# Reordering a software-pipelined attention slot: transposes first, values and division ahead of the last products, norms ahead of the scores

## The chip, the core and the metric

The kernel runs on one core of a Trainium2 chip. The metric is device time in microseconds (us) of one execution, from the launch to the end, as the median of several runs. A profile of one execution goes with it: its span runs from the first to the last instruction.

Five engines work side by side, each through its own instructions in the order in which the kernel wrote them: TensorE (PE; its weight loads, PEld, overlap its matmuls), VectorE (DVE), ScalarE (ACT), GpSimd (POOL) and SyncE (SP), which here issues nearly all DMAs. An instruction that waits holds everything behind it on its engine.

## What is computed

The reference takes x of shape (8, 512, 128) in fp32 and has two parts.

1. A recurrence over the 512 positions, `h = tanh(h A' + x_t B')`, `y = h C'`, whose output is normalised and added to x.
2. Six layers, each an attention and a feed-forward part, each with a residual. The attention has 16 heads of width 64. Queries and keys are scaled to length one, multiplied with learned scales and rotated (rotary embedding with a scale). Every window of 32 queries looks at its own 32 keys and the 32 before them:

```
sim  = einsum('bhwie,bhwje->bhwij', bq, bk2) * 8.0      # 32 x 64 per window, masked
attn = softmax(sim, -1)
out  = einsum('bhwij,bhwje->bhwie', attn, bv2)          # then @ Wo
```

The feed-forward part centres and normalises x, forms `hg = xn @ W1 + b1` with 2 x 341 columns, and adds `(a * gelu(gate)) @ W2 + b2`.

## The kernel before

**Groups.** A group is 8 heads of one batch row (two groups per row, 16 per layer, 96 in all); in layer 0 it is 8 heads of one chunk of 128 positions of four batch rows. `GP = 4` pairs of heads make a group's 128x512 tiles.

**Slots.** The main loop (L1073 to L1097) walks over groups n and, within a group, over four slots t = 0 to 3, one for each 128 query positions. `slot(n, t, feed)` (L952) writes out by hand what every engine does, for several groups at once. `cur` is group n, `one` is n+1, `two` is n+2, `old` is n-1. `last` is the quarter before (t-1 of `cur`, or quarter 3 of `old`), and `back` is the quarter two before.

A quarter of `cur` goes through these steps:

- `mask` (L613): ACT copies the mask into the two PSUM banks `sc`, one quarter ahead.
- `scores` (L623): 64 small PE matmuls add the products of queries and keys to it.
- `less_max` (L636, L639): DVE takes the row maximum and subtracts it into `e` (one buffer).
- `exps` (L646): ACT, in place in `e`.
- One slot later, `turn` (L652, L657): PE transposes `e` into `tp`, ACT copies it to `eT` (one buffer).
- `average` (L670): 64 PE matmuls of `eT` with the values (with a column of ones) into two banks `av`.
- `divide` (L687, L688): DVE takes the reciprocal of the row sum and multiplies, into `ao` (one buffer).
- Another slot later, `turn_back` (L699, L703): PE transposes `ao` into `at`, ACT copies it to `aoT`.
- At t = 1 of the next group, `project` (L708) multiplies all of `aoT` with Wo into `yo`, and `add` (L719) adds it to x.

**Pieces of the groups to come** fill the gaps between these steps. They stand in five lists `fill[0]` to `fill[4]`, which `run(0)` to `run(4)` call:

- t = 0: `one.sums` (L426, `nsq`: sums of squares, then the DVE step x at L441) in `run(0)`; `one.values(0)` and the ten-step reciprocal root `one.inv.solve()` (L446 to L452, DVE) in `run(1)`; `values(1)` in `run(2)`; `values(2)` in `run(3)`. `values` is PE L583 and the ACT copy L592 into `vbuf`.
- t = 1: `one.spread` (L461, `bc`: the reciprocal roots spread over the partitions, four banks) and `one.finish(0)` (DVE L561, then four DMAs on SP) in `run(1)`; `finish(1)` to `finish(3)` later; `old.project` in `run(3)`.
- t = 2 and t = 3: two units of `two`, each `unit_a` (PE L522 `rawa`, ACT L526, DVE L512) and `unit_b` (PE L534 `rawb`, ACT L538 and L540, then POOL L544 and L545); at t = 3 also `one.values(3)` in `run(4)`.

**PSUM.** The pool `mm` has four banks (three during the recurrence); `nsq`, `bc`, `yo`, `rawa`, `rawb`, `vps` and the feed-forward tiles take them in turn. `tp`, `at` and the two `av` take turns in two banks of the pool `acc` (L168). So `tp` waits until `divide` has read the first `av` of the slot before, `at` until it has read the second, and `av` in turn until ACT has copied `tp` and `at`.

**Feed-forward.** Eleven of the groups carry a `Feed` over four batch rows in their slots: `centre` (L828) at t = 0, `sums` and `inv.solve` at t = 1, `apply` (L856) at t = 2. `apply` spreads the roots (`bc_f`), scales four tiles (L859) and then runs the matmuls `fa`, `fg` (L879, L883), the Gelu (ACT L891), the product (DVE L897) and `yf` (L905). A last Feed stands behind the groups.

**Recurrence.** Until group `NREC = 9` the 512 steps of the recurrence run beside the groups: every helper ends in `rec.tick(us)`, which puts one step (a PE matmul L291, an ACT tanh L299) into both queues when enough work has passed. `rec.need` runs the remaining steps of a chunk alone where a group needs its result. There `exps` stands behind `run(2)`, and the fourth `bc` is made after the first three, for want of a bank.

Of the kernel before, what the change touches and what calls it, by code (L numbers as in the profile page):

```python
# [48 lines left out]
def mk_seq_preln_kernel(  # L49
# [112 lines left out]
    with tc.tile_pool(name="qk", bufs=2) as qkp, tc.tile_pool(  # L162
# [634 lines left out]
        class Feed:  # L797
# [55 lines left out]
                        c = slice(3 * h + k, 3 * h + k + 1)  # L853
                        nc.vector.tensor_add(self.b1[:kn, c], bp[:kn, c], self.b1[:kn, c])

            def apply(self):  # L856
                bcs = self.inv.spread(range(GP), f"f{self.nm}")
                for j in range(GP):
                    nc.vector.scalar_tensor_tensor(  # L859
                        self.ctr[j],  # L860
                        bcs[j],
                        par_sb[:, self.l, 4:5],
                        self.ctr[j],
                        ALU.mult,
                        ALU.mult,
                    )
                prs = {}
                for j in range(GP):
                    for k in range(len(KC)):
                        self.hidden(j, k, prs)  # L870
                        if k == 0 and j > 0:
                            self.output(j - 1, prs)
                self.output(GP - 1, prs)
# [53 lines left out]
        NREC = 9  # L927
# [3 lines left out]
        def begin(n):  # L931
            nonlocal xs
            l, b, g = todo[n]
            buf = (n // 2) % 2
            if l == 0:
                c, h = b
                if g == 0:
                    rec.need(c)
                    xs = shifted_chunk(c, h, buf)
                groups[n] = ChunkGroup(n, c, h, g, xs)  # L940
                return
            if n < GL + 4 and g == 0:
                nc.vector.memset(xbufs[buf][D // 2 :, WINDOW : WINDOW + 1], 0.0)
            if g == 0:
                xs = shifted(b, buf)
            groups[n] = Group(n, l, b, g, xs)
# [5 lines left out]
        def slot(n, t, feed=None):  # L952

            cur, one, two = groups.get(n), groups.get(n + 1), None
            old = groups.get(n - 1)
            if n + 2 < len(todo):
                if t == 1 or n + 2 not in groups:
                    begin(n + 2)  # L960
                two = groups.get(n + 2)
            last, lt = (cur, t - 1) if t > 0 else (old, NT - 1)
            back, bt = (cur, t - 2) if t > 1 else (old, NT - 2 + t)
            fill = [[] for _ in range(5)]
            if one and t == 0:
                fill[0] = [one.sums]
                fill[1] = [lambda: one.values(0), lambda: one.inv.solve()]
                fill[2] = [lambda: one.values(1), lambda: one.between(0)]
                fill[3] = [lambda: one.values(2)]
            if feed and t == 0:  # L970
                fill[4] = fill[2] + fill[3]
                fill[2] = [lambda: feed.centre((0, 1))]
                fill[3] = [lambda: feed.centre((2, 3))]
            if one and t == 1:
                fill[1] = [lambda: one.spread(range(4)), lambda: one.finish(0)]
                if n < NREC:

                    fill[1] = [lambda: one.spread((0, 1, 2)), lambda: one.finish(0)]
                    fill[2] = [lambda: one.spread((3,))]
            if feed and t == 1:  # L980
                fill[0] += [feed.sums]
            if old and t == 1:
                fill[3] = [lambda: old.project(wo)]
            if two and t >= 2:
                u = 2 * t - 4
                fill[0] = [lambda: two.unit_a(u)]
                fill[1] = [lambda: two.unit_b(u)]
                fill[2] = [lambda: two.unit_a(u + 1)]
                fill[3] = [lambda: two.unit_b(u + 1)]
            if one and t == 3:  # L990
                fill[4] = [lambda: one.values(3), lambda: one.between(1)]
            if feed and t == 2:
                fill[4] = fill[2] + fill[3]
                fill[3] = fill[1]
                fill[2] = fill[0]
                fill[0], fill[1] = [], [lambda: one.values(3), lambda: one.between(1)]
            if feed and t == 3:
                fill[4] = []

            def run(k):  # L1000
                for f in fill[k]:
                    f()
                if t != 1 or k == 0:
                    rec.piece()
                elif k < 4:
                    rec.piece(False)

            run(0)
            if cur:
                cur.scores(t)  # L1010
            if last:
                last.turn(lt)
            if back:
                back.turn_back(bt)
            run(1)
            if feed and t == 2:
                feed.apply()
            if cur:
                cur.less_max(t)
            if feed and t == 1:  # L1020
                feed.inv.solve()
            if cur and n >= NREC:
                cur.exps()
            run(2)
            if cur and n < NREC:
                cur.exps()
            if cur and t + 1 < NT:
                cur.mask(t + 1)
            elif one and t == NT - 1:
                one.mask(0)  # L1030
            if one and t == 1:
                one.finish(1)
            if last:
                last.average(lt)
            if one and t == 1 and not feed:
                one.finish(2)
                one.finish(3)
            run(3)
            if last:
                last.divide(lt)  # L1040
            if feed and t == 1:
                one.finish(2)
                one.finish(3)
            run(4)
            if old and t == 1:
                old.add()
            if one and t == 3 and renew(n + 1):
                l, _, g = todo[n + 1]
                wv[g] = load_v(l + 1, g)
            if two and t == 3 and renew(n + 2):  # L1050
                l, _, g = todo[n + 2]
                wqk[g] = load_qk(l + 1, g)
            if one and t == 3 and one.l == 0:
                one.keep()

        with tc.manual_schedule():
            ahead = rec.first(0)
            for f in ahead:
                f()
            ahead = [f for c in range(1, NT) for f in rec.first(c)]  # L1060
            while rec.t < P:
                if rec.t % 8 == 7 and ahead:
                    ahead.pop(0)()
                rec.step()
            for _ in range(2):
                rec.piece()
            while rec.posted == 0:
                rec.piece()
                rec.step()
            for t in (2, 3):  # L1070
                slot(-2, t)
            feed = soon = None
            for n in range(-1, len(todo) + 1):  # L1073
                m, l = n % GL, n // GL
                if n == NREC:
                    rec.need(NT - 1)
                    recs.close()
                    mmp = mms.enter_context(tc.tile_pool(name="mm", bufs=4, space=PSUM))
                    ffn_w = load_ffn_weights(0)
                for t in range(NT):  # L1080
                    if t == 3 and n < len(todo) - 1:
                        if n == 12 or (m == 8 and l > 0):
                            soon = Feed(l, 0, ffn_w)
                            soon.biases()
                            biases = soon.b1
                            soon.shift()
                        if m == 0 and l > 0:
                            soon = Feed(l - 1, GP, ffn_w)
                            soon.b1 = biases
                            soon.shift()  # L1090
                    slot(n, t, feed)
                    if feed and t == 2 and feed.b0 == GP:
                        ffn_w = load_ffn_weights(feed.l + 1)
                feed, soon = soon, None
                old = groups.pop(n - 1, None)
                if old and old.n % GL == GL - 1 and old.n + 1 < len(todo):
                    wo = load_wo(old.l + 1)  # L1097
            feed = Feed(DEPTH - 1, GP, ffn_w)
            feed.b1 = biases
            feed.shift()  # L1100
            feed.centre(range(GP))
            feed.sums()
            feed.inv.solve()
            feed.apply()

        for b in range(B):
# [114 lines left out]
```

## Time and profile before

| what | value |
|---|---|
| median of three runs | 3921.19 us (3915.84 to 3924.16) |
| the profiled execution's own time | 3917.3 us |
| its span | 3915.5 us, 158605 instructions |
| mean granted TensorE clock | 0.970 |
| DVE busy | 2543.4 us (65%), 5208 instructions |
| ACT busy | 1933.8 us (49%), 3864 instructions |
| POOL busy | 1825.3 us (47%), 780 instructions |
| HBM read and written | 34.56 MB and 14.20 MB |

How to read the profile lines: in a timeline, a line has the start (us from the span's start), the time, the engine, the source line, the operation, output and input by the program's names with the buffer numbers left out, and how many instructions are merged. In brackets stands the idle time of the engine ahead of the line and what ended it. Names with c0h to c3h belong to layer 0. A PE line's time includes the drain of its last matmul, so that the step from one line's start to the next line's start is what a group of matmuls takes.

### The profile page before, as it was taken

What the parts mean: (1) busy time and instruction counts of PE and PEld (TensorE: products, weight loads), DVE (VectorE), ACT (ScalarE), POOL (GpSimd) and SP (SyncE); (2) the same over time, 40 slices, a digit from 0 to 9 for tenths busy, and PEclk for the clock granted to TensorE, in tenths of its full rate; (3) what the DMA queues carried; (4) which work ended last, traced back from release to release, by engine and by line L of the source; (5) the groups of instructions that cost most, each with busy time, mean ns of one, the idle gap of its engine ahead of it and who ended that gap; (6) DMA issues with size and microseconds to landing.
All of it is one profiled execution on the core that took longest, in us unless ns stands there. A gap on an engine that the chain in (4) does not pass through costs nothing.

```text
span 3915.5 us, 158605 instructions
## 1 busy us (share of the span) xinstructions
PE 3536.6 (90%) x69816; PEld 2164.5 (55%) x69816; DVE 2543.4 (65%) x5208; ACT 1933.8 (49%) x3864; POOL 1825.3 (47%) x780
## 2 busy tenths in 40 slices
PE   5797987999999999999999999999999999999997
PEld 4565655555555555555555455555555555555553
DVE  3355565766677677677677677577677677677673
ACT  1253443545455455455455455455455455455452
POOL 0152341535365356366366366366365355355350
PEclk9897987999999999999999999999999999999998
DMA  3152433554345355355345345255345355354342
GB/s 108 28 116 64 110 79 78 123 128 92 86 113 118 72 117 129 85 113 120 68 112 134 78 109 119 66 117 132 76 111 117 69 128 123 77 118 111 74 110 60
DMA packets 366076, 390.50 MB, mean 100 GB/s; under 512 B 96846, under 2 KB 262220, under 8 KB 365260
## 3 DMA queue, kind: packets, MB, share of 16 engines
q1 hardware_dynamic: 364380, 378.09, 42.2%
q8 instruction: 551, 9.03, 1.0%
q10 hardware_dynamic: 1008, 2.27, 0.2%
q14 instruction: 137, 1.12, 0.1%
HBM read 34.56 MB, written 14.20 MB: 12 GB/s over the span
## 4 chain that ended last, share of the span: by engine, by line
PE 69%; DVE 17%; ACT 8%; issue 4%; DMA 2%; SPq 1%; ACTq 0%; DVEq 0%; POOL 0%
PE sc L623 6%; PE yo L708 6%; PE rawb L534 5%; PE vps L583 5%; PE tp L652 5%; PE rawa L522 5%; PE xb L291 4%; PE nsq L426 4%; PE at L699 4%; PE fa L879 3%; PE yf L905 3%; DVE t L561 3%; PE fg L883 3%; DVE t L512 3%; PE av L670 2%
## 5 line engine op out<-in xcount | busy, mean ns | idle before, releaser
L544 POOL TENSOR_TENSOR u<-rope_sb,bs 128x1024 f32<-128x1024 f32 x320 | 765.9, 2394 | 1347.2 <-ACT bs L540 1168.7
L545 POOL TENSOR_TENSOR t<-t,u 128x1024 f32<-128x1024 f32 x320 | 756.9, 2365 | 25.1
L561 DVE TENSOR_TENSOR t<-t,bc 128x1024 f32<-128x1024 f32 x320 | 376.4, 1215 | 286.8 <-PE bc L461 286.7
L512 DVE SCALAR_TENSOR_TENSOR t<-rawa,par_sb,rope_sb 128x1024 f32<-128x1024 f32 x320 | 409.6, 1280 | 203.3 <-ACT sq L526 196.6
L646 ACT ACTIVATE e<-e 128x512 f32<-128x512 f32 x320 | 201.7, 630 | 432.7 <-DVE e L639 318.2
L657 ACT COPY eT<-tp 128x512 f32<-128x512 f32 x320 | 187.6, 586 | 454.2 <-PE tp L652 454.2
L623 PEld LDWEIGHTS sc<-kbuf,qT 64*32 64x32 f32 x20480 | 226.4, 105 | 257.5 <-ACT sc L613 161.8
L623 PE MATMUL sc<-kbuf,qT 64*32 64x64 f32 x20480 | 280.4, 224 | 85.5 <-ACT sc L613 83.4
L534 PE MATMUL rawb<-xbuf,wqk 128*128 128x512 f32 x640 | 343.9, 619 | 0.0
L708 PE MATMUL yo<-aoT,wo 128*128 128x512 f32 x640 | 298.4, 609 | 35.4 <-DVE t L561 34.3
L522 PE MATMUL rawa<-xbuf,wqk 128*128 128x512 f32 x640 | 328.3, 594 | 1.7 <-DVE t L512 1.7
L583 PE MATMUL vps<-wv,xbuf 128*64 128x256 f32 x2560 | 329.7, 389 | 0.0
L670 PEld LDWEIGHTS av<-vbuf,eT 64*32 64x32 f32 x20480 | 226.9, 105 | 180.5 <-ACT sq L538 110.7
L291 PEld LDWEIGHTS xb<-hT,s1w 128*128 128x128 f32 x1022 | 202.8, 237 | 186.6 <-ACT hT L299 128.6
L670 PE MATMUL av<-vbuf,eT 64*32 64x65 f32 x20480 | 283.4, 225 | 13.0 <-issue 9.8
L688 DVE TENSOR_TENSOR ao<-av,rc 128x256 f32<-128x256 f32 x640 | 271.8, 425 | 22.0
L291 PE MATMUL xb<-hT,s1w 128*128 128x8 f32 x1022 | 223.3, 291 | 57.1 <-ACT hT L299 57.1
L526 ACT ACTIVATE sq<-rawa 128x512 f32<-128x512 f32 x320 | 190.4, 595 | 152.9 <-PE rawa L522 152.9
L299 ACT ACTIVATE hT<-xb 128x8 f32<-128x8 f32 x512 | 91.9, 179 | 329.2 <-PE xb L291 313.7
L652 PE MATMUL tp<-ident,e 128*128 128x128 f32 x1280 | 206.1, 284 | 44.1 <-DVE rc L687 43.2
L583 PEld LDWEIGHTS vps<-wv,xbuf 128*64 128x64 f32 x2560 | 162.4, 136 | 139.5 <-issue 64.4
L639 DVE TENSOR_TENSOR e<-sc,mx 128x512 f32<-128x512 f32 x320 | 221.4, 692 | 27.6 <-PE rawa L522 0.5
(280 smaller groups left out, 6176.4 us busy)
## 6 DMA issues: line engine op xcount, KB each, us to landing
qT<-t SPq DMA_DIRECT2D x640, 128.0 KB
kbuf<-t SPq DMA_DIRECT2D x640, 128.0 KB
vbuf<-vbuf SPq DMA_DIRECT2D x544, 130.0 KB
vbuf<-vbuf SPq DMA_DIRECT2D x160, 97.5 KB
xbuf<-xT SPq DMA_DIRECT2D x95, 128.0 KB
xbuf<-xT SPq DMA_DIRECT2D x80, 127.8 KB
wqk<-in_w_qkv SPq DMA_DIRECT2D x12, 512.0 KB
xf<-xT SPq DMA_DIRECT2D x24, 256.0 KB
```

Of the source, the lines that this page charges most:

```text
L291: nc.tensor.matmul(self.xb[:, k, :], abc[:, 0, :], self.hT[:, (t - 1) % P, :], start=False, stop=True, skip_group_check=True,)
L512: nc.vector.scalar_tensor_tensor(t, self.twice(raw), scale, self.rope(isk, 1), ALU.mult, ALU.mult)
L522: nc.tensor.matmul(raw, self.wqk[:, c, 0], self.xs[:, WINDOW:], start=True, stop=True)
L534: nc.tensor.matmul(raw, self.wqk[:, c, 1], self.xs[:, WINDOW:], start=True, stop=True)
L544: nc.gpsimd.tensor_mul(self.wide(u), self.rope(isk, 0), self.twice(bs))
L545: nc.gpsimd.tensor_add(self.ts[c], self.ts[c], u)
L561: nc.vector.tensor_mul(t, t, self.bcs[c].unsqueeze(1).to_broadcast([P, 2, S]))
L583: nc.tensor.matmul(ps[par * KB : (par + 1) * KB, j], self.xs[:, k0 : k0 + KB], self.wv[:, par * GP * DH : (par + 1) * GP * DH], start=True ...
L623: nc.tensor.matmul(self.sc[blk * QB : (blk + 1) * QB, par, i, :], self.qT[rows, i, q0 : q0 + QB], kT[rows, i, :], start=False, stop=True, ...
L652: nc.tensor.transpose(tp[:, i, :], self.e[:, i].rearrange("p a k -> p (a k)"), ident)
L670: nc.tensor.matmul(av[blk * QB : (blk + 1) * QB, i, :VW], self.eT[rows, i, blk * QB : (blk + 1) * QB], self.v[rows, BT * t + blk, i, :], s ...
L708: nc.tensor.matmul(self.yp, wo[:, self.g * GP + c, :], self.aoT[:, c, :], start=(c == 0), stop=(c == GP - 1),)
```

## The change

The steps of a slot are put into another order, and the Feed's `apply` is cut into `scale` (spread and scaling) and `apply` (the matmuls).

- `turn` and `turn_back` come first, ahead of `run(0)` and `scores`.
- `average`, `less_max`, `exps` and `divide` follow `run(1)`; before, `average` stood behind `run(2)` and `divide` behind `run(3)`.
- At t = 1, `spread` and `finish(0)` move from `run(1)` to `run(0)`, ahead of the scores; `finish(1)` comes behind `divide`.
- In a group with a Feed, `feed.sums` moves from `run(0)` to `run(2)` at t = 1, with `inv.solve` behind it; at t = 2 `feed.scale` is `run(0)` and `feed.apply` is `run(3)`, behind `less_max`, `exps`, `average` and `divide` of that slot, which before stood behind it or around it.

```diff
-            def apply(self):
+            def scale(self):
                 bcs = self.inv.spread(range(GP), f"f{self.nm}")
                 for j in range(GP):
                     nc.vector.scalar_tensor_tensor(
...
+
+            def apply(self):
                 prs = {}
...
             if one and t == 1:
-                fill[1] = [lambda: one.spread(range(4)), lambda: one.finish(0)]
-                if n < NREC:
-
-                    fill[1] = [lambda: one.spread((0, 1, 2)), lambda: one.finish(0)]
+                cs = (0, 1, 2) if tight else range(4)
+                fill[0] = [lambda: one.spread(cs), lambda: one.finish(0)]
+                if tight:
                     fill[2] = [lambda: one.spread((3,))]
             if feed and t == 1:
-                fill[0] += [feed.sums]
+                fill[2] += [feed.sums]
...
             if feed and t == 2:
-                fill[4] = fill[2] + fill[3]
-                fill[3] = fill[1]
-                fill[2] = fill[0]
-                fill[0], fill[1] = [], [lambda: one.values(3), lambda: one.between(1)]
+                fill[4] = fill[0] + fill[1] + fill[2] + fill[3]
+                fill[0], fill[1] = [feed.scale], []
+                fill[2] = [lambda: one.values(3), lambda: one.between(1)]
+                fill[3] = [feed.apply]
...
-            run(0)
-            if cur:
-                cur.scores(t)
             if last:
                 last.turn(lt)
             if back:
                 back.turn_back(bt)
+            run(0)
+            if cur:
+                cur.scores(t)
             run(1)
-            if feed and t == 2:
-                feed.apply()
+            if last:
+                last.average(lt)
             if cur:
                 cur.less_max(t)
-            if feed and t == 1:
-                feed.inv.solve()
-            if cur and n >= NREC:
-                cur.exps()
+                if not tight:
+                    cur.exps()
+            if last:
+                last.divide(lt)
+            if one and t == 1:
+                one.finish(1)
             run(2)
-            if cur and n < NREC:
+            if cur and tight:
                 cur.exps()
             if cur and t + 1 < NT:
                 cur.mask(t + 1)
             elif one and t == NT - 1:
                 one.mask(0)
+            if feed and t == 1:
+                feed.inv.solve()
             if one and t == 1:
-                one.finish(1)
-            if last:
-                last.average(lt)
-            if one and t == 1 and not feed:
                 one.finish(2)
                 one.finish(3)
             run(3)
-            if last:
-                last.divide(lt)
-            if feed and t == 1:
-                one.finish(2)
-                one.finish(3)
             run(4)
```

Here `tight` stands for `n < NREC`. Behind the last group, `feed.scale()` is called ahead of `feed.apply()`.

## The prediction

> **What bounds the kernel now.** I read the page's shares of busy time first, then the chain that ended last, then the timeline of one ordinary group, engine by engine.
>
> ```profile
> PE 3536.6 (90%) x69816; PEld 2164.5 (55%) x69816; DVE 2543.4 (65%) x5208; ACT 1933.8 (49%) x3864; POOL 1825.3 (47%) x780
> PE 69%; DVE 17%; ACT 8%; issue 4%; DMA 2%; SPq 1%; ACTq 0%; DVEq 0%; POOL 0%
> ```
>
> TensorE is the bound, with waits on DVE and ACT strung into its chain. An order can only win those waits. Where they lie shows the PE timeline of one ordinary group (the projection's start recurs every 30.90 us, 1203.98 to 1234.88):
>
> ```profile
> 1199.63 0.86 PE L623 MATMUL sc<-kbuf,qT 64*32 64x64 f32 x64 [1.12 <-ACT sc L613]
> 1201.44 1.17 PE L461 MATMUL bc<-k,selt_sb 32*128 32x128 f32 x32
> 1203.98 3.70 PE L708 MATMUL yo<-aoT,wo 128*128 128x512 f32 x8 [0.57 <-DVE t L561]
> 1207.52 1.02 PE L522 MATMUL rawa<-xbuf,wqk 128*128 128x512 f32 x2
> 1213.92 1.02 PE L522 MATMUL rawa<-xbuf,wqk 128*128 128x512 f32 x2
> 1216.14 0.63 PE L652 MATMUL tp<-ident,e 128*128 128x128 f32 x4 [0.42 <-DVE rc L687]
> 1221.83 1.95 PE L426 MATMUL nsq<-sq,sel_sb 128*32 128x128 f32 x64
> ```
>
> Slots begin at 1199.63 (t=1), 1207.52 (t=2), 1213.92 (t=3), 1221.83 (t=0). They last 7.89, 6.40, 7.91 and, until the next t=1 at 1230.53, 8.70. Three waits, 1.12 + 0.57 + 0.42 = 2.11 us, leave 28.8 of pure TensorE work. The longest comes from a chain over DVE and ACT in t=0:
>
> ```profile
> 1223.86 0.29 DVE L441 TENSOR_SCALAR x<-nsq 128x128 f32<-128x128 f32 x1 [1.04 <-PE nsq L426]
> 1227.31 0.68 DVE L636 TENSOR_REDUCE mx<-sc 128x8 f32<-128x512 f32 x1
> 1228.10 0.69 DVE L639 TENSOR_TENSOR e<-sc,mx 128x512 f32<-128x512 f32 x1
> ```
> ```profile
> 1228.88 0.63 ACT L646 ACTIVATE e<-e 128x512 f32<-128x512 f32 x1 [1.62 <-DVE rc L687]
> 1229.42 0.57 ACT L592 COPY vbuf<-vps 128x512 f32<-128x512 f32 x1
> 1229.88 0.59 ACT L613 CAST sc<-mask_sb 128x512 f32<-128x512 bf16 x1
> ```
>
> The sums of squares start at 1221.83. x follows 2.03 later, ten steps of the root, the maximum, the subtraction, and the exponential 7.05 after the sums' start. A copy and the mask stand behind it, and only then may the next scores start.
>
> **The ordinary group, slot by slot.** No instruction is added or removed; only waits and orders change. Steps below are differences of starts in these timelines.
>
> *t=0.* The two transposes (0.55 + 0.50) now stand ahead of the sums, so the whole chain is 1.05 later: exponential at 8.10, end 8.73. The next slot starts with `tp`, which needs the exponential, not the mask: it starts at about 8.80 instead of 8.70. TensorE's own work in the slot is 7.45, so a wait of 1.35 takes the place of the mask's 1.12: **+0.10**.
>
> *t=1.* Transposes 1.03, `bc` 1.11, scores 0.80, `av` 0.80, projection 3.50. `bc`'s fourth bank holds the values copied last: ACT's queue (exponential, copy 0.54 later, mask 0.47, copy 0.52, 0.59 long) frees it 1.4 after the slot's start, where `bc` wants it at 1.24, so 0.2 is lost. `finish(0)` starts 1.26 after `bc` and ends at 3.7; the projection wants its bank at 3.94, so the 0.57 is gone. Sum 7.45 against 7.89: **-0.44**. What is late next is DVE: `finish(0)`, maximum, subtraction, division, three more `finish` of 1.13 and the addition end at 10.05, which is 2.6 into t=2.
>
> *t=2.* TensorE's work is 6.38 (`tp` 0.55, `at` 0.46, units 0.95 + 0.95 + 0.86 + 0.95, scores 0.85, `av` 0.80). `rawa` starts at 1.02; its square on ACT 1.05 later, DVE's product 0.63 after that, at 2.70 (DVE is free at 2.6). The maximum follows 1.20 later, the subtraction 0.78, the exponential 0.79, ending at 6.10. The next `tp` comes at 6.38, 0.28 later. No wait, **-0.02**, but this margin is the plan's thinnest place.
>
> *t=3.* ACT now carries two squares, a scaling, a mask behind each exponential and is free 1.7 into t=3, so `eT` and the square of `rawa` come 0.7 later than in t=2 and the exponential ends at 6.8. The values' product of 1.0 makes this slot 7.48 long, which covers it. The wait of `tp` for the division (0.42) is gone, since the division now ends in its own slot: **-0.43** against 7.91.
>
> Sum 30.11 against 30.90, -0.79 a group. Groups 9 to 93 without a Feed are 74: **-58 us**. SP gets its DMAs in the same order, `finish(0)`'s earlier in the slot; POOL's four units (4.75 each) stay within 24 us of the 30, so neither queue ends a wait.
>
> **The groups with a Feed** (eleven). Before, from sums to sums, 71.26 (1284.31 to 1355.57):
>
> ```profile
> 1301.30 3.70 PE L708 MATMUL yo<-aoT,wo 128*128 128x512 f32 x8 [0.57 <-DVE t L561]
> 1307.47 0.63 PE L652 MATMUL tp<-ident,e 128*128 128x128 f32 x4 [1.68 <-DVE rc L687]
> 1312.58 1.12 PE L879 MATMUL fa<-xf,w 128*128 128x512 f32 x2 [0.64 <-DVE xf L859]
> 1316.68 1.09 PE L879 MATMUL fa<-xf,w 128*85 128x512 f32 x2 [0.40 <-ACT gl L891]
> ```
>
> Now four things stand in each other's way. Counting from the slot's `tp`:
> 1. The exponential at 8.10 has nine copies of ACT behind it (before: at 7.05). The last values' copy ends at 14.1, and `bc`, moved ahead, waits for that bank: it ends at 15.0.
> 2. `finish(1)` stands behind the division and starts at 18.7, so the projection, which takes its bank, starts at 20.0 instead of 17.0: **+3.0**, a wait of 2.0 for the 0.57 shown.
> 3. `feed.scale` takes the bank of the projection, so it waits for `finish(2)`, `finish(3)` and the addition, until 26.2; from there scaling, scores, `av`, values, and `fa` at 30.2. From the projection's end to `fa` it is 6.7 against 7.65 (1304.93 to 1312.58): **-1.0**.
> 4. The exponential, a copy and the mask now stand on ACT ahead of the Gelu's table and first two Gelus; the fifth matmul pair waits for them 1.65 instead of 0.40: **+1.2**. Behind the Feed a slot without scores and `av` is 0.8 shorter: **-0.8**.
>
> Sum +2.4, times 11: **+26 us**.
>
> **The recurrence** (about nine groups). Before, TensorE runs gapless but for one place:
>
> ```profile
> 344.35 1.15 PE L461 MATMUL bc_c0h<-k_c0h,selt_sb 32*128 32x128 f32 x8 [1.05 <-DVE t_c0h L561]
> 346.87 2.05 PE L708 MATMUL yo_c0h<-aoT_c0h,wo 128*128 128x512 f32 x2
> ```
>
> That 1.05 goes (scores and `av` stand between), but the projection now waits for `finish(1)` behind the division, some 2 us: together nothing. In t=2 and t=3 the exponential stands behind the second square, and the next slot's `tp` needs it 8.2 after the slot's start, where TensorE is there at 7.96. The tanh of the steps queue behind that backlog: 0.24 + 0.57 + 0.4, about 1.2 a group: **+11 us**.
>
> Total -58 + 26 + 11 = -21: 3917.3 becomes 3896.3. The median of the runs lies 3.9 above the profiled execution, so **3900 us**.
>
> **Unknown costs.** A `tp` that waits directly for an exponential is in no row; from below it costs nothing (margin 0.28 holds), from above what `tp` waits elsewhere, 1.68, per slot. I take nothing, as ACT and DVE rows give the ends to 0.1. For the Feed I bound from -0.6 (the 0.57 goes as in ordinary groups) to +4.5 (waits 2 and 4 with no credit for 3); I take the sum. For the recurrence 0 to 2.2 (a wait as long as the projection's in each group).
>
> **A rule that speaks against it.** The granted clock was 1.00 from 1307 to 1313 us, behind the wait of 1.68 and eight transposes, and 0.50 in the empty stretch 304 to 327. The Trainium skill, page "TensorE: Matmul & The Clock Gate", sections "What's actually happening" and "Part 4: PE-mode transpose", says that the clock halves after an idle window of about 3.4 us and that transposes don't count as work. The new order puts waits right against transposes: 1.35 + 1.05 in each group stays under the window, the Feed's `tp`, `at` and wait for banks come near it. By the rule a lost window would cost up to 1.7 us, an estimate from that page, eleven times 19. The row shows none, and my sum has none.
>
> **Rivals.**
> - *B, the Feed loses little* (1 instead of 2.4) and the recurrence nothing: -58 + 11 = -47, 3874. For it: the waits in the Feed overlap, and PE has 1.68 to give. Against: the bank order is fixed.
> - *C, all is given back*: the Feed costs 4, the recurrence 2.2 a group: -58 + 44 + 20 = +6, 3927. This is also the case in which the change does not do what it says: the wait on the mask comes back under the name of the exponential.
> - *D, slower*: ACT's queue in t=2 and t=3 is the new bound. ACT carries ten operations, about 5.3 us, in a slot of 6.4, in order, between a DVE chain of 5.3. Every delay beyond 0.28 in t=2 makes `tp` wait, which delays `eT`, the next square, the next maximum. At 0.6 beyond it, 74 groups lose 44: +23, 3944. It decides from 0.3 beyond, where the total crosses zero. For it: ACT's rows show waits for DVE of 318 us at the exponential. Against: every step above was taken from a row.
>
> **Chances.** Forecast 0.45 (3885 to 3913), B 0.20 (3860 to 3885), C 0.15 (3913 to 3929), D 0.20 (above). A measurement tells 0.2%, 7.8 us. Faster is the forecast with B, 0.65; same is C, 0.15; slower is D, 0.20. The range for 8 in 10 reaches from B's 3868 to D's 3938.
>
> **What would show it.** Right: `sc` has no wait on L613 at t=1; `tp` there waits about 1.3 for the exponential (L646); `yo` and the `tp` of t=3 have no wait in ordinary groups; the projections lie 30.1 apart; in Feed groups `yo` waits about 2 for L561 and group time is near 73.7. Wrong: `tp` waits at the start of t=3 (then D), or a granted clock under 1.00 in the Feed groups, or a period of 30.5 and more.

## The result and the profile after

The changed kernel takes 3943.77 us (median, 3938.76 to 3947.89) where the kernel before took 3918.52 in the same series (3912.38 to 3924.16). The ratio is 1.0064, 95% interval 1.0043 to 1.0085: **slower by 0.6%**, where 3900 and faster was forecast, and 6 us beyond the top of the range. The profiled execution took 3945.58, span 3943.8, mean clock 0.972 (before 0.970).

The page of the changed kernel, its shares of busy time and its chain:

```profile
PE 3555.5 (90%) x69816; PEld 2196.7 (56%) x69816; DVE 2565.5 (65%) x5208; ACT 1902.9 (48%) x3864; POOL 1825.3 (46%) x780
PE 71%; DVE 15%; ACT 6%; issue 6%; DMA 1%; SPq 1%; POOL 0%; DVEq 0%; ACTq 0%
```

DVE and ACT have given up 4 points of the chain, as the change wants it. But "issue", time in which TensorE waits for nothing that the profile shows, went from 4 to 6%. Which instructions it falls on stands in the page's groups: the V products, first in the kernel before, then after (the last columns are the idle time ahead of the group and what ended most of it).

```profile
L670 PE MATMUL av<-vbuf,eT 64*32 64x65 f32 x20480 | 283.4, 225 | 13.0 <-issue 9.8
```
```profile
L670 PE MATMUL av<-vbuf,eT 64*32 64x65 f32 x20480 | 302.1, 225 | 56.7 <-issue 55.9
```

Between 1000 and 3880 us TensorE idles for 197 us before and 185 after (the same stretch of time, not of work: the changed kernel is up to 30 us behind in it). Gone are the mask (82 to nothing), the division (43 to 1), most of `finish` (34 to 13). In their place stand the exponential (76.5) and issue (11 to 76).

An ordinary group of the changed kernel in which nothing is missing, TensorE's timeline (start, time, ...; the order of the last `sc` and the first `av` is blurred because modelled ends overlap):

```profile
1237.54 1.95 PE L426 MATMUL nsq<-sq,sel_sb 128*32 128x128 f32 x64
...
1245.20 0.66 PE L652 MATMUL tp<-ident,e 128*128 128x128 f32 x4 [1.15 <-ACT e L646]
1245.69 0.60 PE L699 MATMUL at<-ident,ao 128*128 128x128 f32 x4
1246.22 1.61 PE L461 MATMUL bc<-k,selt_sb 32*128 32x128 f32 x32
1247.76 0.80 PE L623 MATMUL sc<-kbuf,qT 64*32 64x64 f32 x60
...
1248.42 0.91 PE L670 MATMUL av<-vbuf,eT 64*32 64x65 f32 x62
1249.26 3.70 PE L708 MATMUL yo<-aoT,wo 128*128 128x512 f32 x8
```

This is what the prediction drew: no wait of `sc` for the mask, 1.15 of `tp` for the exponential, none of `yo`. From its sums to the next it is 29.96 (30.11 was forecast, 30.89 is the median before; the shortest is 29.93). The group ahead of it, in the same stretch:

```profile
1215.30 1.61 PE L461 MATMUL bc<-k,selt_sb 32*128 32x128 f32 x32
...
1217.50 0.43 PE L670 MATMUL av<-vbuf,eT 64*32 64x65 f32 x21
1218.71 0.67 PE L670 MATMUL av<-vbuf,eT 64*32 64x65 f32 x41 [0.78 <-issue]
1219.31 1.13 PE L708 MATMUL yo<-aoT,wo 128*128 128x512 f32 x2
```

From `bc` to `yo` 4.01 instead of 3.04, for the same instructions. Of 69 ordinary groups behind 930 us 42 are of this kind ("stalled" below; the others "clean"); the stretch takes 3.00 to 3.07 in the clean ones and 3.46 to 5.07 in the stalled ones, 47.5 us over 3.03 in all.

| from the sums of one group to those of the next, summed | before | after | difference | forecast |
|---|---|---|---|---|
| sums behind the recurrence start at | 665.1 | 676.5 | +11.4 | +11 |
| 11 groups with a Feed | 793.1 | 806.5 | +13.4 | +26 |
| 75 ordinary groups | 2331.7 | 2337.3 | +5.6 | -58 |
| the end, behind the last sums | 125.5 | 123.4 | -2.1 | 0 |

The error is in the third row: it is 64 us off, of which the Feed groups give 13 back. Had all 75 been as long as the shortest, it would be -72 (75 x (29.93 - 30.89)).

**What "issue" is.** The table of DMA queues has one for TensorE's instructions (packets, MB, share of 16 engines):

```profile
q8 instruction: 551, 9.03, 1.0%
```

9.03 MB in 551 packets are 16 KB each. The trace has 141025 records of TensorE (matmuls, weight loads, semaphore waits); over 551 that is 256 a packet. So the instructions come in blocks of 256, that is 128 matmuls with their weight loads. Two facts of the trace tie the waits to these packets. Of the 64 issue waits over 0.5 us between 1000 and 3880 us, 61 end 1.1 to 1.8 us after the end of such a packet (median 1.39), and all 11 in the kernel before do. And no two packets of the queue start less than 3.28 us apart in any of the 14 traces, though the 128 matmuls of `sc` and `av` back to back, with their weight loads as many instructions as a packet holds, take 1.6.

The Trainium skill has the frame: page "Runtime: NRT & Kernel Launch", section "Instruction fetch mechanics", says that the instructions are refilled in blocks of 16 KB, 256 instructions, by a DMA queue that the engine's sequencer drives while it executes the block before, and that this is mostly hidden. Blocks, their size and the queue agree with the trace; that it is hidden does not hold here.

In the kernel before, the transposes stood between the scores and the V products:

```profile
1200.42 0.66 PE L652 MATMUL tp<-ident,e 128*128 128x128 f32 x4
1200.91 0.60 PE L699 MATMUL at<-ident,ao 128*128 128x128 f32 x4
1201.44 1.17 PE L461 MATMUL bc<-k,selt_sb 32*128 32x128 f32 x32
1202.55 0.86 PE L670 MATMUL av<-vbuf,eT 64*32 64x65 f32 x64
```

**Theory T1**: from `bc` to the last `av`, 320 instructions now stand back to back and take 2.7 us. That is faster than instructions arrive, so if a block ends in an unlucky place, TensorE runs dry. **T2**: the fetch is slow because of the DMAs that `finish(0)` now starts at this moment. **T3**: rival D of the prediction, ACT's queue is the bound and issue is a side effect.

### The profile page after: what moved, and what is told of

The parts are those of the page before. It is cut to its first block, busy times and chain, and to the rows that moved or that the text cites. A ratio compares the mean times of both kernels' runs of the same rounds, so it can differ in the third digit from the quotient of the medians.

```text
span 3943.8 us, 158206 instructions
## 1 busy us (share of the span) xinstructions
PE 3555.5 (90%) x69816; PEld 2196.7 (56%) x69816; DVE 2565.5 (65%) x5208; ACT 1902.9 (48%) x3864; POOL 1825.3 (46%) x780
## 3 DMA queue, kind: packets, MB, share of 16 engines
q8 instruction: 551, 9.03, 1.0%
## 4 chain that ended last, share of the span: by engine, by line
PE 71%; DVE 15%; ACT 6%; issue 6%; DMA 1%; SPq 1%; POOL 0%; DVEq 0%; ACTq 0%
PE rawa L522 7%; PE rawb L534 7%; PE yo L708 6%; PE sc L623 5%; PE av L670 4%; PE tp L652 4%; PE xb L291 4%; PE nsq L426 4%; PE at L699 3%; PE bc L461 3%; PE yf L907 3%; PE vps L583 3%; PE fa L881 3%; PE fg L885 3%; DVE e L639 2%
## 5 line engine op out<-in xcount | busy, mean ns | idle before, releaser
L670 PEld LDWEIGHTS av<-vbuf,eT 64*32 64x32 f32 x20480 | 239.5, 105 | 205.8 <-issue 155.1
L670 PE MATMUL av<-vbuf,eT 64*32 64x65 f32 x20480 | 302.1, 225 | 56.7 <-issue 55.9
L522 PE MATMUL rawa<-xbuf,wqk 128*128 128x512 f32 x640 | 342.8, 617 | 0.0
L708 PE MATMUL yo<-aoT,wo 128*128 128x512 f32 x640 | 306.7, 623 | 18.6 <-issue 8.9
L652 PEld LDWEIGHTS tp<-ident,e 128*128 128x128 f32 x1280 | 145.5, 141 | 233.1 <-ACT e L646 144.5
L592 ACT COPY vbuf<-vps 128x512 f32<-128x512 f32 x320 | 186.4, 588 | 176.1 <-PE vps L583 176.1
L538 ACT ACTIVATE sq<-rawb 128x512 f32<-128x512 f32 x320 | 190.7, 596 | 142.8 <-PE rawb L534 142.2
```

What stands on the lines that cost most here:

```text
L522: nc.tensor.matmul(raw, self.wqk[:, c, 0], self.xs[:, WINDOW:], start=True, stop=True)
L652: nc.tensor.transpose(tp[:, i, :], self.e[:, i].rearrange("p a k -> p (a k)"), ident)
L670: nc.tensor.matmul(av[blk * QB : (blk + 1) * QB, i, :VW], self.eT[rows, i, blk * QB : (blk + 1) * QB], self.v[rows, BT * t + blk, i, :], s ...
L708: nc.tensor.matmul(self.yp, wo[:, self.g * GP + c, :], self.aoT[:, c, :], start=(c == 0), stop=(c == GP - 1),)
```

## The experiments

Medians of 4 to 6 runs, ratio to the kernel before of the same series with its 95% interval. "Ordinary" is the mean of 69 groups (sums to sums), "best" the shortest of them, "issue" TensorE's issue waits between 1000 and 3880 us. The diffs of the experiments are shortened; conditions such as "only from group 9 on" or "not in groups with a Feed" stand in the expectations.

| kernel | us | ratio to before | ordinary (best) | issue |
|---|---|---|---|---|
| before | 3918.52 | 1 | 30.96 (30.89) | 11 |
| changed | 3943.77 | 1.0064 (1.0043 to 1.0085) | 30.96 (29.93) | 76 |
| e1_split_project | 3964.32 | 1.0117 (1.0097 to 1.0137) | 31.28 (31.01) | 34 |
| e2_close_t0 | 3962.06 | 1.0109 (1.0088 to 1.0130) | 31.14 (29.95) | 75 |
| e3_old_rec | 3944.03 | 1.0062 (1.0044 to 1.0080) | 31.08 (29.94) | 75 |
| e4_old_feed | 3966.61 | 1.0124 (1.0103 to 1.0144) | 30.94 (29.72) | 64 |
| e5_spread_early | 3853.91 | 0.9826 (0.9810 to 0.9842) | 29.75 (29.09) | 42 |
| e6_early_split | 3854.81 | 0.9830 (0.9814 to 0.9845) | 29.78 (29.30) | 35 |
| e7_shift | 3952.45 | 1.0078 (1.0061 to 1.0095) | 31.02 (29.92) | 76 |
| e8_early_split_old_rec | 3847.52 | 0.9809 (0.9791 to 0.9826) | 29.76 (29.30) | 31 |
| e9_values_between | 3836.55 | 0.9776 (0.9760 to 0.9793) | 29.60 (29.30) | 24 |
| e10_spread_behind_scores | 3956.45 | 1.0083 (1.0068 to 1.0098) | 31.13 (30.24) | 79 |
| e11_feed_finish | 3846.79 | 0.9806 (0.9792 to 0.9820) | 29.76 (29.31) | 27 |
| e12_at_between | 4036.73 | 1.0292 (1.0275 to 1.0310) | 32.31 (31.34) | 14 |

**e1, the run cut in two.**

```diff
-    fill[0] = [one.spread(range(4)), one.finish(0)]
-    fill[3] = [old.project(wo)]
+    fill[0] = [one.spread((0, 1, 2)), one.finish(0)]
+    fill[1] = [old.project(wo, (0, 1))]        # ahead of average
+    fill[2] = [old.project(wo, (2, 3)), one.spread((3,))]
```

> The changed kernel, but in ordinary groups (n >= 9, no Feed) half of the projection (yo) stands at t=1 between the scores and the V products, the other half behind these; three of the four bc are spread ahead of the scores and the fourth behind the projection, so that yo finds a free bank. Theory T1 (PE's instructions run out where bc, sc and av stand back to back: 320 records of matmuls and weight loads in 2.7 us): the issue waits between 1000 and 3880 us fall from 76 to below 35, ordinary groups last 30.0 to 30.5 instead of 31.1, the whole 3885 to 3912. T2 (the instruction fetch is slowed by the DMAs that finish(0) starts at that moment, not by the density): issue waits stay above 60 and the time at 3936 to 3952. T3 (ACT's queue in t=2 and t=3 is the bound, as in rival D of the prediction): tp waits at the start of t=3 and t=0 stay, the time at 3936 to 3952 or longer.

The waits went as T1 says: 76 to 34, and of 36 waits of `av` right behind `sc` three are left. The time went the other way, and the timeline shows why:

```profile
1216.47 1.17 PE L461 MATMUL bc<-k,selt_sb 32*128 32x128 f32 x24
1217.57 0.86 PE L623 MATMUL sc<-kbuf,qT 64*32 64x64 f32 x64
1218.36 1.99 PE L709 MATMUL yo<-aoT,wo 128*128 128x512 f32 x4
1220.27 0.86 PE L670 MATMUL av<-vbuf,eT 64*32 64x65 f32 x64
1221.06 1.98 PE L709 MATMUL yo<-aoT,wo 128*128 128x512 f32 x4
1222.98 1.15 PE L461 MATMUL bc<-k,selt_sb 32*128 32x128 f32 x8
```

The 24 `bc` take 1.10 to the next start, as long as all 32 did, and the 8 set apart take 1.08 once more. The four row groups of `bc` run beside each other, so that one alone costs as much as four. That is the experiment's own price: 29.93 + 1.08 = 31.01, its best group. So e1 speaks for T1 by its waits, and its time tells nothing against it.

**e2, another run made dense.** At t=0 the first `vps` goes ahead of the scores, which puts `sc` and `av` together.

```diff
-    fill[0] = [one.sums]
-    fill[1] = [one.values(0), one.inv.solve()]
+    fill[0] = [one.sums, one.values(0)]
+    fill[1] = [one.inv.solve()]
```

> The changed kernel, but at t=0 the first values product (vps) stands ahead of the scores, so that sums (64 matmuls), then 8, then scores and V products (128) stand back to back; nothing is added. T1: at t=0 the issue waits rise from some 13 of 1.0 us to 35 or more, and the whole to 3958 to 3990. T2 (DMAs): t=0 starts no finish; issue waits and time stay, 3936 to 3952. T3: the same, no change.

The time came out as T1 had it, but not for its reason: the issue waits did not rise, 75 against 76. A run of 256 instructions between slower ones, 1.6 us long, made t=0 stall in 15 of 70 groups, no more than the 16 of the changed kernel, while the run of 320 at t=1 stalls in 42. Of the 18 us more, 8 lie ahead of 930 us and 12 in the ordinary groups; what they are is not shown.

**e3 and e4, the old order in the recurrence, and in the Feed groups.** The old `slot` is called where `n < NREC`, or where the group has a Feed.

> The order of before in all groups n < 9 (the recurrence), the changed order behind them. The step of the prediction (+11 for the recurrence): the first sums of 64 matmuls after the recurrence start at 665 instead of 676.5, the whole 3944 - 11 = 3933 (3926 to 3939). Rival: the recurrence is paced by its own chain and regains the loss, 3944.

> The order of before in all four slots of the eleven groups with a Feed, the changed order elsewhere. If the Feed groups lose 13.4 as the two traces say: 3944 - 13 = 3931 (3924 to 3936), each Feed group near 72. If the clean +2.4 of the prediction is the price: 3944 - 26 = 3918. Rival: the issue waits only move into these groups, 3944.

In e3 the first sums behind the recurrence come 9.5 earlier (667.1 against 676.5 in the changed kernel) and those of the first ordinary group behind 930 us 12.0 (938.5 against 950.5): the step is right. But the whole did not move: 8 of it went in the ordinary groups. Their instruction supply is not the reason, since the issue waits are the same, 75 against 76; the waits of `tp` for the exponential rose from 76.5 to 82.7, and the cause of the loss stays open. e4 missed by its seams. Its Feed groups last 74.7, longer than in either kernel, for the old order divides at the end of a slot and the new one begins the next with `tp`, which needs that division. The waits of TensorE in e4 (us in total, times, longest):

```profile
PE tp L652 <- DVE rc L687: 33.1, 20, 1.7
```

So parts of the change that look separate, by slot, are not. e4 says nothing on the price of the new Feed order.

**e7, nothing moved, the blocks shifted.** In one slot, once, the 64 V products are issued twice.

```diff
+    last.average(lt, 2 if (n, t) == (NREC, 3) else 1)   # 2: the same 64 again
```

> The changed kernel; in one slot (n = 9, t = 3) the 64 V products are issued a second time, into the same place: 128 instructions of PE more, 0.8 us, once. Nothing is moved. In the changed kernel the stretch from bc to the projection at t=1 takes 3.03 where the first bc is instruction 32 to 127 of a block of 256 (the instruction fetch moves 16 KB at a time), and 3.4 to 5.1 where it is not. If the place in the block decides (T1): the class of every ordinary group turns over, a group that took 3.03 takes 3.4 or more and the other way round, in 9 of 10 groups; the whole 3936 to 3956. If it is the DMAs of the moment (T2) or anything that goes with the group: the same groups stall as in the changed kernel.

I number TensorE's records from the start and call the number of a group's first `bc`, modulo 256, its place. In the changed kernel an ordinary group has 1406 records, 5 blocks and 126, so that places jump by about half a block from one group to the next: neighbours alternate. The shift moves each group by 128. Two neighbouring groups of e7 (compare the two shown of the changed kernel, where the first stalled and the second did not):

```profile
1231.27 0.87 PE L670 MATMUL av<-vbuf,eT 64*32 64x65 f32 x62
1232.06 3.70 PE L708 MATMUL yo<-aoT,wo 128*128 128x512 f32 x8
...
1262.47 0.45 PE L670 MATMUL av<-vbuf,eT 64*32 64x65 f32 x22
1263.98 0.66 PE L670 MATMUL av<-vbuf,eT 64*32 64x65 f32 x40 [1.06 <-issue]
```

They have changed roles. Of 70 groups behind 900 us, 27 went from stalled to clean and 27 from clean to stalled. The other 16 stalled in both; my 9 of 10 forgot that with a clean zone of 96 places some have a bad place in both kernels. Over both kernels:

| place of the first `bc` | groups | from `bc` to `yo` |
|---|---|---|
| 32 to 127 | 53 | 3.00 to 3.10, all |
| 0 to 31, 128 to 255 | 87 | 3.46 to 5.32, mean 4.2; one of them, at 22, 3.02 |

The same group, with the same DMAs around it, stalls or not by its place alone. This settles T1 against T2.

**e5 and e6, `bc` into the wait for the exponential.** Out of the run, and into the 1.15 us that `tp` waits anyway.

```diff
 # t == 0
+    fill[3] += [one.spread(range(4))]       # end of the slot
-    cur.exps()                              # ahead of run(2)
+    cur.exps()                              # behind run(3), then the mask
 # t == 1
-    fill[0] = [one.spread(range(4)), one.finish(0)]
+    fill[0] = [one.finish(0)]
 # e6 alone, t == 1
+    fill[1] = [old.project(wo, (0, 1))]     # between scores and average
+    fill[3] = [old.project(wo, (2, 3))]
```

> The changed kernel; in ordinary groups the 32 bc are spread at the end of t=0, ahead of the transposes, into the time in which tp waits for the exponential, and the exponential and the mask stand on ACT behind the copies of the values. finish(0) stays first in t=1, finish(1) stands ahead of the division. At t=1, scores and V products still stand back to back. Steps: t=1 loses bc (1.54 with its wait for a bank), the rest stays: 8.80 + 6.2 + 13.9 = 28.9 a group where no instruction is missing. T1 (instruction supply): issue waits at t=1 stay, 25 us or more between 1000 and 3880, mean of ordinary groups 29.2 to 29.7, the whole 3830 to 3865. T2 (DMAs beside the fetch): the same time, but e6 would be 18 longer than this. T3 (ACT or DVE is the bound, rival D): the waits come back as tp waits for L646 or L687 in t=2 and t=3, mean 30.5 or more, 3910 or more.

> As e5, but half of the projection stands between scores and V products at t=1 and half behind them; the split itself costs 0.28 a group (the two halves took 2 x 1.91 in e1, the whole 3.54). T1: no issue wait of av at t=1, those left (t=0, and the groups with a Feed) below 35 us, ordinary groups 29.0 to 29.4, the whole 3815 to 3850 and 0 to 35 below e5 in spite of the split. T2: 18 above e5 (64 x 0.28). T3: 3910 or more.

In both, `finish(1)` also stands ahead of the division at t=1. Both are 2.3% faster than the changed kernel and 1.7% faster than the one before. T3 falls: with TensorE given work in its wait, ACT and DVE deliver at 29.1 a group, so they were no bound at 31. The waits of `tp` for the exponential fell from 76.5 to 10.8. e5 came within the bounds of T1, a little long in the ordinary groups (29.75); e6 missed them, 3854.81 against 3850 at most and 29.78 against 29.4, and is 1 us behind e5 where T1 said 0 to 35 ahead and T2 said 18 behind. Without `bc` the run has 256 instructions, and only 13 of 70 such stretches stall (42 of 70 in the changed kernel), so that the split has little left to win and pays for itself at best.

> As e6, with the order of before for n < 9 (recurrence). The sums behind the recurrence start 11 to 12 us earlier, as e3 showed; the whole is 11 below e6, give or take 8 for other places of the instructions in their blocks. Rival (the gain is lost again behind, as in e3): the same as e6.

e8: the sums come 11.2 earlier than in e6, the whole is 7 shorter, within the bounds given.

**e9, the same cure at t=0.**

```diff
 # t == 0, on top of e8
-    fill[2] = [one.values(1), one.between(0)]
+    fill[1] += [one.values(1), one.between(0)]   # ahead of average
```

> As e8, but at t=0 of ordinary groups two values products instead of one stand between the scores and the V products (the second moved ahead by one place). T1: the issue waits of av behind nsq, sc, vps (9 of 1.0 us in e8, 15 in e5) fall to 3 or fewer, and the time by 5 to 12, to 3836 to 3843. Rival (what limits e8 is no longer the supply): 3847, within 4.

3836.55, 11 less than e8, the time that T1 gave: **the fastest kernel of this study, 0.9776 of the time before** (0.9760 to 0.9793). Of the waits behind `nsq`, `sc`, `vps` eight are left instead of nine, more than I expected, but with 4 us instead of 9: the second `vps` gives the fetch 0.9 more. From t=0 to t=1 TensorE now runs like this:

```profile
1193.67 0.50 PE L461 MATMUL bc<-k,selt_sb 32*128 32x128 f32 x6
1194.42 1.15 PE L461 MATMUL bc<-k,selt_sb 32*128 32x128 f32 x26 [0.26 <-ACT vbuf L592]
1195.51 0.66 PE L652 MATMUL tp<-ident,e 128*128 128x128 f32 x4
...
1196.53 0.86 PE L623 MATMUL sc<-kbuf,qT 64*32 64x64 f32 x64
1197.38 1.98 PE L709 MATMUL yo<-aoT,wo 128*128 128x512 f32 x4
1199.29 0.86 PE L670 MATMUL av<-vbuf,eT 64*32 64x65 f32 x64
```

**e10, one part of the change undone: `bc` behind the scores.**

```diff
+    if not tight:
+        fill[1], fill[0] = fill[0], []
```

> The changed kernel with one part undone: from n = 9 on, spread and finish(0) stand behind the scores again, so that at t=1 the order is transposes, sc, bc, av, yo. T1: 32 bc of 35 ns between sc and av thin out the run as in the kernel before, where 18 waits of 0.5 were left; the issue waits between 1000 and 3880 us fall from 76 to 20 to 45; yo waits again about 0.5 for finish(0), 0.8 later than in the changed kernel, and bc no longer waits 0.44 for its bank: mean of ordinary groups 30.3 to 30.7, the whole 3905 to 3930. T2 (DMAs): finish(0)'s DMAs come 0.8 later, the stalls move with them and stay, 3944 and more.

```profile
1216.45 0.86 PE L623 MATMUL sc<-kbuf,qT 64*32 64x64 f32 x64
1217.24 1.17 PE L461 MATMUL bc<-k,selt_sb 32*128 32x128 f32 x32
1218.35 0.42 PE L670 MATMUL av<-vbuf,eT 64*32 64x65 f32 x23
1219.31 0.66 PE L670 MATMUL av<-vbuf,eT 64*32 64x65 f32 x41 [0.54 <-issue]
```

My expectation was wrong for T1: 79 us of issue waits, and the time 3956, the figures that T2 had (e7 speaks against T2 all the same). The run is `sc`, `bc`, `av` now, the same 320 instructions in 2.7 us; 43 of 70 stall. What stands in the middle does not matter. In the kernel before, `tp` and `at` stood in it: 336 instructions in 3.7 us, and 19 of 70 stretches stalled, 10 us in all. TensorE's order at t=1 differs between e10 and the kernel before in the transposes alone. So the part of the change that brings the stalls is, by this comparison, that the transposes left the run, not that `bc` moved. The best group is 30.24, since `yo` waits for `finish(0)` again, as expected.

**e11, a step of the prediction for the Feed groups.** In e8's Feed groups, `finish(1)` goes right behind `finish(0)`.

```diff
+    if feed:
+        fill[0] += [one.finish(1)]      # t == 1, no longer behind the division
```

> As e8, but in groups with a Feed finish(1) stands right behind finish(0), ahead of the maximum, so that the projection does not wait behind the division (step 2 of the prediction, a wait of 2.1). If this wait is the price of the Feed groups: 11 x 1.6 = 18 less than e8, 3829. If DVE's chain up to the addition is (it runs without a gap from the first finish to the addition, 11 us, and feed.scale waits for its end; step 3): the yo wait goes, the group time stays at 73.4, the whole 3847, within 5.

3846.79 against 3847.52, Feed groups 73.7 against 73.4, and the waits of 2.1 of `yo` are gone: the wait of `yo` was not the price. It only stands ahead of DVE's chain, which runs without a gap from the first `finish` to the addition and ends where it ended.

**e12, the transposes back into the run.**

```diff
-    back.turn_back(bt)                      # ahead of run(0)
+    if t != 1 or tight: back.turn_back(bt)
     run(0)
     cur.scores(t)
+    if t == 1 and not tight: back.turn_back(bt)
```

> The changed kernel, but at t=1 (n >= 9) the four transposes at stand between the scores and the V products, as half of them stood inside this run in the kernel before. e10 showed that it does not matter where bc stands in the run: 320 instructions of PE (bc, sc, av with their weight loads) in 2.7 us outrun the instruction fetch, of which no two packets (256 instructions) started less than 3.3 us apart. If the length in time of the run decides: sc, at and av now take 2.1 for 272 instead of 1.6 for 256, the run with bc 3.2 or, with the wait of av for aoT, up to 3.8; the issue waits between 1000 and 3880 us fall from 76 to 25 to 50. The time moves little, 3925 to 3950: bc waits up to 0.5 longer for its bank, and av waits up to 0.7 for ACT's copy of at (L703). If instead only the number of instructions since the last wait decides, nothing changes: 70 us or more of issue waits.

The issue waits fell to 14, further than expected. The time went to 4037, far beyond what I allowed for. The best group is 1.41 longer (`bc` waits for its bank, `av` for ACT's copy), which I had in part. The rest I put down to the clock. Window sums of one group, at t=0 and in `sc` and `at` of t=1 (window, its length, busy us and instructions of PE, PEld, DVE, ACT and POOL, granted clock, DMA share, GB/s):

```profile
2414.00:2423.00 9.00, 7.79 (x229) 5.55 (x225) 6.36 (x18) 4.16 (x9) 8.84 (x5) 1.00 0.38 84
2425.70:2427.90 2.20, 2.20 (x70) 1.67 (x69) 1.86 (x3) 0.00 (x0) 0.00 (x0) 0.50 0.92 211
```

Between 930 us and the last sums the trace of e12 has 28 stretches at a granted clock of 0.50, 150 us in all; the changed kernel has 5 with 17 us, the kernel before 3 with 17. If TensorE does half as much in them, the added 133 us cost about 66, an estimate. This confounds the test: a slower clock also gives the fetch more time. What holds is that with 14 us of issue waits left a group is no shorter; where the waits go is shown by e7, not here.

## Why the prediction was wrong

- **Ordinary groups, -58: wrong, and this is the failed step.** The waits went as said. Where nothing stalled, the length of the slots was right, 8.68, 7.60, 6.28 and 7.40 for t=0 to 3 in the clean group above, from `tp` to `tp` (8.80, 7.45, 6.38 and 7.48 were forecast). What failed is the sentence "No instruction is added or removed; only waits and orders change": I took the time of `bc`, `sc` and `av`, 1.11 + 0.80 + 0.80, from rows in which transposes stood between them, and added them up for a place where they stand back to back. In that place TensorE's instructions do not arrive fast enough, and 42 of 69 groups stall. The row that should have warned was there, 17 issue waits of `av` in the kernel before, up to 1.1 us; I read the 4% of issue in the chain and gave it no cause. Measured price: 47.5 us in the stretch from `bc` to `yo`. Another 24 (69 x (30.96 - 29.93) - 47.5) lies elsewhere in these groups: issue waits at t=0 (15 us) and waits of `tp` for the exponential outside t=1 (14 us) are of that size; how they share it is not shown.
- **Feed groups, +26: half of it.** The order of waits was right (`bc` 2.56 long, `yo` 2.10, `fa` 1.37 in the changed kernel below), the group time too, 73.3 against 73.7. The base was off: I took 71.26, which six of the eleven take, but the mean before is 72.1, since four others (72.67 to 74.54) each hold a stretch at a granted clock of 0.50. Shortest against shortest the price is 1.7 (73.00 against 71.26), by the means 1.2. And step 2 was no cost of its own, as e11 shows.

```profile
1897.67 2.56 PE L461 MATMUL bc<-k,selt_sb 32*128 32x128 f32 x32
...
1905.04 3.67 PE L708 MATMUL yo<-aoT,wo 128*128 128x512 f32 x8 [2.10 <-DVE t L561]
...
1919.99 1.09 PE L881 MATMUL fa<-xf,w 128*85 128x512 f32 x2 [1.37 <-ACT gl L893]
```

- **Recurrence, +11: right,** 11.4 between the traces, 9.5 to 12.0 by e3.
- **Rival D, slower, gave the sign and the size, but not the mechanism.** Waits of `tp` for the exponential outside t=1 are 14 us between 1000 and 3880 us, not 44, and e5 shows that ACT's queue is no bound. That its 3944 was met is luck. The thin margin of 0.28 held in most groups.
- **The rule that speaks against it** did not decide: over the whole run the changed kernel has 223 us at a granted clock of 0.50, the one before 233. The sign "a granted clock under 1.00 in the Feed groups" came in four of the eleven, for 3.4 us each, but the kernel before has four such groups too. In e12 the clock did fall, see below.

## What to carry to other kernels

Time for a run of tiny matmuls is only what the row says as long as instructions keep up; before they are moved together, set their number and time against what the fetch delivers (here 256 in 3.3 us at best). Read "issue" as a wait with a cause: look for the instruction queue among the DMA queues, and at where the packets end. And where an engine must wait for another, look for work that is ready and can fill that wait, rather than for an order that moves the wait: e5, which does this, is 2.3% faster than the changed kernel. The shortest groups (29.93 and 29.09) put some two thirds of that on the filled wait, an estimate; the rest is fewer stalls. The reordering alone cost 0.6%.

## What the runs showed of the hardware that was not expected

- TensorE's instructions come in packets of 16 KB (256 instructions), never less than 3.28 us apart in these traces, taking 0.9 to 1.9 us, mostly 1.2; a stalled engine goes on about 1.4 us after the packet's end. 64 pairs of weight load and matmul of 64x64 take 0.80 us, so that a block can be used up in 1.6.
- Whether a run of 320 instructions stalls depends on its place in the blocks. 64 products issued once at the ninth group turned over 54 of 70 groups behind it, so that an edit ahead of a run also decides which of the later runs stall. On the whole this evened out in e7, 1.0078 of the time before against 1.0064, with intervals that overlap.
- 8 `bc` of one row group take 1.08 us, 32 of four row groups 1.10.
- In e12 the clock went to 0.50 for 3.4 or 6.8 us at a time, in the group shown from 2425.2 on. Ahead of that stand a wait of `tp` of 1.22, four transposes, six `bc` and a wait of 0.40:

```profile
2422.95 0.66 PE L652 MATMUL tp<-ident,e 128*128 128x128 f32 x4 [1.22 <-ACT e L646]
2423.53 0.50 PE L461 MATMUL bc<-k,selt_sb 32*128 32x128 f32 x6
2424.43 1.38 PE L461 MATMUL bc<-k,selt_sb 32*128 32x128 f32 x26 [0.40 <-ACT vbuf L592]
```

The Trainium skill, page "TensorE: Matmul & The Clock Gate", section "Part 4: PE-mode transpose", says that transposes do not count as busy for the gate in the way other matmuls do. Within e12 that agrees: in the 3.41 us ahead of each of the 28 stretches, matmuls other than transposes fill 0.35 to 0.47 of the time, and in all other such windows between 930 us and the last sums 0.46 or more. But the changed kernel kept a clock of 1.00 in windows in which they fill 0.31 to 0.34. So no run here shows what the gate counts.
